# Moving stores, loads and receives between the steps of a one-core decoder kernel, and one layer-norm operand

## The chip, the cores and the metric

The kernel runs on one core of one Trainium2 chip. The metric is the device time of one execution in microseconds. Before the change three runs took 1194.85, 1200.84 and 1200.17 us, a median of 1200.17 us. The work is in float32 throughout.

A core has five engines with an instruction stream each: TensorE (PE, matmuls into PSUM), VectorE (DVE), ScalarE (ACT), GpSimd (POOL) and SyncE (SP). In this kernel nearly all DMA transfers are issued from SP. Each engine carries out its stream in order; semaphores hold an instruction until what it needs is there.

## What is computed

The input is 16 sequences of 128 tokens with 512 features (`x`) and 16 context sequences of the same size. First comes a decoder layer, then a gated cross attention to the same context. Both have 16 heads of 32 features. Cut to what matters:

```python
# decoder layer
ln_out = layernorm(hidden_states, ln1_s, ln1_b)
q, k, v = jnp.split(ln_out @ w_qkv + b_qkv, 3, axis=-1)
x = hidden_states + merge_heads(attention(q, k, v, ltor_mask)) @ w_ao + b_ao
q = layernorm(x, ln2_s, ln2_b) @ w_q + b_q
k, v = jnp.split(encoder_states @ w_kv + b_kv, 2, axis=-1)
x = x + merge_heads(attention(q, k, v, cross_mask)) @ w_co + b_co
x = x + gelu(layernorm(x, ln3_s, ln3_b) @ w1 + b1) @ w2 + b2
# gated cross attention
a = layer_norm(audio_kv, gamma, beta)          # audio_kv is the context
Q, K, V = x @ Wq.T, a @ Wk.T, a @ Wv.T         # 16 heads
out = softmax(Q K^T * scale, masked) @ V
return x + tanh(gate) * (out @ Wo.T)
```

## The kernel before

**Groups and sections.** The 16 sequences are four groups (`GB = 4` sequences each). There are twelve attention sections: A0 to A3 (self attention), B0 to B3 (cross attention to the context) and D0 to D3 (gated). The MLP of the decoder lies between B3 and D0. `x[g]` stays in SBUF for each group.

**Steps.** `attend` (line 634) runs the sections in steps, 16 to a section, four to a sequence. One step handles one unit: four heads (one of each chunk of 128 features) of one sequence. A unit passes through several steps: at step k its scores are scaled and masked (DVE, POOL), at k+1 come the row minimum (DVE) and the exponentials (ACT), at k+2 the normalization (`norm_unit`, POOL), at k+3 the DVE transposes 32x32 blocks and the unit is sent to DRAM (`turn_unit`, tile `away`). Two units make a pair; `receive_pair` (line 581) reads a pair back in four pieces so that the blocks land transposed (tile `pT`). This happens at the start of each even step, two steps after the pair's second unit was sent. When a sequence's two pairs are back, `mix` multiplies with the values (matmuls `av`) at step 4m+2; the first pair has been received four steps before that, the second two. The output projection (`mo`) follows two steps later for A and B. For D0 to D2 it is put off (`deferred`): the mixed values `mT` are kept, in DRAM for D0 and D1 (`put_away`), and multiplied beside the last section.

**What else a step holds.** The `jobs` of a step are pieces of other work, above all the projections of the next section. The dictionary or list that stands beside them says in which step each comes. `ahead.prepare(p)` is work for the section after the next, one call a step. `afterwards(engine, do)` puts a piece off to the start of the next step, where `due()` carries out all such pieces, DVE's first. A piece that puts off another moves that by one step more. All instructions are kept in program order on their engine (class `InOrder`), so the position in the program is the position in the queue, SP's included. All instructions carry line 49 in the profile for this reason; they are told apart by their tiles.

**Turning through DRAM.** Layer-normalized activations are turned in the same manner as the softmax results: DVE transposes blocks, SP sends them to DRAM (`turned_...`), and `receive` (line 254) reads them back in four pieces of 256 KB (`back_...`), two at once and two at the next `due()`. `chunk_back` (ACT) then scales one chunk of 128 features into place.

**Layer norm.** `normalize` (line 206) takes mean and variance (DVE), the inverse root (`rstd`, a 128x1 power on POOL), then, other than at the start, an offset `off = -mean * rstd` of one value per partition (DVE, line 224) and one ACT instruction that scales and shifts. There are 56 such offsets in the program.

**The stages that the change touches.**
- B3 (the last cross group) has as its jobs what `beside_last_cross` (line 1487) lists: the key and value projections of the first gated group with stores of the results (`key_job`, `value_job`), layer norm for the MLP (`mlp_start`, tiles `ln_C`, `turned_C`, `back_C`), twelve loads of MLP weights in pieces of 256 KB, and the first pieces of the MLP.
- The MLP's pieces are numbered by `n` (0 to 16) and `r` (0 to 6). `beside_mlp` adds work for the gated sections, in the last two `n` the preparation of D1 through `gates[1].prepare`.
- In D0 to D3 `GatedAttention.prepare` (line 1300) receives the turned `x` and the turned, normalized context `a` of the section after the next, scales them into place, lets POOL make the sums that the seven-product block multiplication needs (`x_sums`), and, while D0 runs, turns and sends the hidden states of group 3 (`hidden_states`) and adds a term to them (`add_void`).
- Beside D2 `deferred_start` (line 1416) fetches the kept `mT` of D0 and D1 (`mixed`) and the first group's `x` (`x0`), which had been stored to use its place for sums.

**Buffers.** The tag `ln` has one buffer, which `ln_tile` and the received tiles share in turn; `pT` has three; `mT` has one.

Of the kernel before, what the change touches and what calls it, by code (L numbers as in the profile page):

```python
# [25 lines left out]
GB = 4  # L26
# [26 lines left out]
def decoder_then_gated_cross_attention(ctx: ExitStack, tc: tile.TileContext, a: dict, out: bass.AP):  # L53
# [152 lines left out]
    def normalize(src, dst, name, then):  # L206

        mv = work.tile([P, 2], F32, tag="mv", name=f"mv_{name}", bufs=4)
        st = work.tile([P, 6], F32, tag="st", name=f"st_{name}", bufs=4)
        nc.vector.bn_stats(st, src)  # L210
        nc.vector.bn_aggr(mv, st)
        rstd = work.tile([P, 1], F32, tag="rstd", name=f"rstd_{name}", bufs=4)
        nc.vector.tensor_scalar(rstd, mv[:, 1:2], EPS, None, ALU.add)
        nc.gpsimd.tensor_tensor(rstd, rstd, mhalf[:, 0:1], ALU.pow)

        def rest():
            to, of = (by_chunk(dst), squares(src)) if len(dst.shape) == 4 else (dst, src)
            nc.vector.tensor_scalar(to, of, mv[:, 0:1], rstd, ALU.subtract, ALU.mult)
            then()

        def rest_by_act():

            off = work.tile([P, 1], F32, tag="off", name=f"off_{name}", bufs=4)
            nc.vector.scalar_tensor_tensor(off, mv[:, 0:1], -1.0, rstd, ALU.mult, ALU.mult)
            nc.scalar.activation(by_chunk(dst), squares(src), AF.Identity, bias=off, scale=rstd)
            afterwards("dve", then)

        afterwards("dve", rest if at_start[0] else rest_by_act)
# [24 lines left out]

    def receive(name, away):

        t = work.tile([P, NQ, GB, KC, Q], F32, tag="ln", name=f"back_{name}")

        def part(m):
# [3 lines left out]
            )  # L262

        for m in range(2):
            part(m)
# [368 lines left out]
    def attend(sections, ready, others, after=None):  # L634
# [15 lines left out]
        def step(k, bt=None, jobs=(), ahead=None):  # L650
# [10 lines left out]
            if projected and (m == 0 or ready and bt is None):  # L661
                before = projected.popleft()
                if before.sec.deferred:
                    before.sec.put_away(before)
                else:
                    out_project(before)
# [274 lines left out]
    def mlp_start(ml):  # L941
# [17 lines left out]
        def start():  # L959
# [5 lines left out]
        return (  # L965
            ([start, row_difference, lambda: ml_receive(0)], [0, 5, 6]), (sends, [0, 1, 2, 3]), (back, [10, 11, 12, 13])
        )
# [4 lines left out]
    def ml_receive(g):  # L972
        ml.back = receive(f"C{g}", ml.away)

# [3 lines left out]
    def mlp(ml, last_steps):  # L978
# [158 lines left out]
        for n in range(len(steps) + 1):  # L1137
# [6 lines left out]
            if n < len(steps):  # L1144
# [11 lines left out]
                elif g + 1 < NG and i == 2:  # L1156
                    lnT = turned_tile(g + 1)
                    at_[0].append(lambda: ml_receive(g + 1))
                    for c in range(KC):
                        at_[3 + c].append(  # L1160
# [101 lines left out]
    def gated_start(first):  # L1262
# [4 lines left out]
        def key_job(c):  # L1267
            project_chunk(first_k, w["gk"], first.aT, c, "k_D0")
            afterwards("act", lambda: keep_part("k_D0", first_k, c))

        def value_job(b):
            values_chunk(first_v, w["gv"], first.aT, b, "v_D0")
            afterwards("act", lambda: keep_part("v_D0", first_v, b))

# [5 lines left out]
    class GatedAttention(Section):  # L1280
# [19 lines left out]
        def prepare(self, p):  # L1300

            g = self.g
            if g == 2 and p == 0:
                self.ln = ln_tile("D3")
            if g == 2 and p < GB:
                gates[3].hidden_states(p, self.ln[:, p])
            elif g == 2 and p < 2 * GB:
                gates[3].add_void(p - GB)
            if p == 5:
                self.back = receive(f"x{g}", self.x_away)  # L1310
                self.xT = act_tile(self.name, "actT" if g == 3 else "enc")
            elif p in (8, 9):
                self.take_hidden(range(2 * (p - 8), 2 * (p - 7)))
            elif p == 10:
                self.back = receive(f"a{g}", self.a_away)
                self.aT = act_tile(f"a{g}", "actT" if g == 1 else "enc")
                self.x_sides, self.x_sums = right_blocks(self.xT, self.x_at)
            elif p >= 14:
                group_back(self.aT, self.back, "gamma", "beta", range(2 * (p - 14), 2 * (p - 13)))
            if p >= 10 and self.x_sums:  # L1320
# [95 lines left out]
        def deferred_start(self):  # L1416
# [13 lines left out]
            def tokens(g, t):  # L1430
# [7 lines left out]
            return (  # L1438
                ([lambda g=g, n=n: fetch_mixed(g, n) for g in range(2) for n in range(KC)], [6, 7, 8, 9, 10, 11, 12, 13]),
                ([lambda n=n: nc.sync.dma_start(out=x[0][:, n], in_=gated["x0"][:, n]) for n in range(GB)], [8, 9, 10, 11]),  # L1440
                ([begin_sums], [11]),
# [4 lines left out]
        def deferred_jobs(self):  # L1446
# [6 lines left out]
            def product(g, n):  # L1453
# [8 lines left out]
            send = lambda g, b: nc.sync.dma_start(out=out[g * GB + b], in_=x[g][:, b, :])  # L1462
            return (
                ([lambda g=g: add_later(g) for g in (1, 2) for _ in range(4)], [0, 1, 2, 3, 8, 9, 9, 10]),
                *blocks_plan(later, DEFERRED_BLOCKS),
# [21 lines left out]
    def beside_last_cross():  # L1487
# [5 lines left out]
        at_ = [0, 8, 10, 12, 14, 15, 15, 16, 16, 17, 18, 19, 19, 20, 21, 21, 22, 23, 23]  # L1493
        loads = [1, 3, 4, 5, 8, 9, 10, 11, 12, 13, 15, 16]
        return plan(
# [9 lines left out]
    def beside_mlp(n, r):  # L1505
# [17 lines left out]
        elif n == nth - 1 and r == 2:  # L1523
# [4 lines left out]
            sec.take_hidden()  # L1528
            gates[1].prepare(5)
        elif n == nth:  # L1530
# [15 lines left out]
            if r < KC:  # L1546
                project_chunk(sec.q, w["gq"], sec.xT, r, "q_D0", bank="mm0")
            for p in {0: (8, 9, 10), 1: (11,), 2: (12,), 3: (13,), 6: (14, 15)}.get(r, ()):
                gates[1].prepare(p)
# [39 lines left out]
```

## Time and profile before

| what | value |
|---|---|
| median of three runs | 1200.17 us |
| the profiled execution, its own time | 1197.73 us |
| its span, first to last instruction | 1195.9 us |
| mean granted TensorE clock | 0.993 |
| bytes moved by DMA | 253.70 MB, 212 GB/s in the mean |
| TensorE busy, 500 to 600 us (end of B3, start of the MLP) | 90.70 of 100 us |
| TensorE busy, 600 to 950 us (MLP) | 348.82 of 350 us |
| TensorE busy, 950 to 1195.9 us (gated sections) | 228.04 of 245.9 us |

The page lists busy time of each engine. Beside it the trace can be asked for each engine's instructions in order of time. Such a row gives the start in microseconds, the duration, the engine, the operation, the tile written and the tiles read, the shape, the number of instructions merged into the row, and in brackets the idle time in front of it with the instruction that ended it. "SPq" rows are DMA issues; their duration is the issue alone and not the transfer. "PEclk" is the clock that TensorE was granted, as a share of full speed. TensorE's timeline over the MLP and most of A and B shows little idle time; most of it lies in the first 90 us, between 520 and 600 us, and after 970 us.

### The profile page before, as it was taken

To read this page: it belongs to the slowest core of one execution; us is meant where nothing else is said; L and a number is where in the kernel's file an instruction comes from. 1 tells how busy PE (TensorE), PEld (TensorE's weight loads), DVE (VectorE), ACT (ScalarE), POOL (GpSimd) and SP (SyncE) were. 2 spreads that over 40 slices of the span, in tenths; PEclk is the share of its full clock that TensorE was granted. 3 is DMA by queue.
4 is the path that set the end of the run, shared out by engine and by line. 5 is a ranking of instruction groups with operands and counts; after the bars stand their busy time and mean duration, and the time that the engine had idled before them with its cause. 6 is when DMAs were issued, how large, how long until landed. Compare 5 with 4: busy or idle time off the path is not lost.

```text
span 1195.9 us, 21040 instructions
## 1 busy us (share of the span) xinstructions
PE 1152.9 (96%) x7010; PEld 830.0 (69%) x7010; DVE 770.5 (64%) x1493; ACT 593.6 (50%) x2061; POOL 673.4 (56%) x612
## 2 busy tenths in 40 slices
PE   7989999999999999988999999999999989999998
PEld 5867777644444444445788888888888767777775
DVE  7678979776867767865745534453441268777773
ACT  2456767666655656654332233232222238766663
POOL 6778878675757566675223523443342257544873
PEclk9999999999999999989999999999999999999999
DMA  6588979998979979797696494587447718888874
GB/s 213 155 193 212 236 197 217 231 269 200 207 215 206 235 196 242 181 257 221 220 330 193 144 306 152 177 266 263 150 161 247 220 40 230 224 226 239 247 204 159
DMA packets 321796, 253.70 MB, mean 212 GB/s; under 512 B 83156, under 2 KB 279960, under 8 KB 316824
## 3 DMA queue, kind: packets, MB, share of 16 engines
q1 hardware_dynamic: 321648, 252.34, 74.6%
q8 instruction: 56, 0.92, 0.3%
q14 instruction: 52, 0.43, 0.1%
q10 hardware_dynamic: 40, 0.01, 0.0%
HBM read 161.06 MB, written 91.23 MB: 211 GB/s over the span
## 4 chain that ended last, share of the span: by engine, by line
PE 82%; DVE 5%; DMA 4%; POOL 3%; issue 3%; SPq 2%; ACT 1%; ACTq 0%; DVEq 0%; POOLq 0%
PE o L49 15%; PE h L49 14%; PE mo_A L49 5%; PE mm_v_B L49 5%; PE mm_q_B L49 5%; PE mm_k_B L49 5%; PE mo_B L49 4%; PE mm_k_A L49 3%; PE mm_q_D L49 3%; PE mm_k_D L49 3%; PE mm_v_A L49 3%; PE mm_v_D L49 3%; PE mm_o_D L49 3%; PE mm_q_A L49 3%; SPq L49 2%
## 5 line engine op out<-in xcount | busy, mean ns | idle before, releaser
L49 ACT ACTIVATE s_B<-s_B,mn_B 128x128 f32<-128x128 f32 x256 | 99.5, 391 | 78.5 <-issue 59.6
L49 DVE TENSOR_TENSOR h<-h,h 128x512 f32<-128x512 f32 x80 | 54.9, 686 | 114.3 <-PE h L49 113.7
L49 ACT ACTIVATE s_A<-s_A,mn_A 128x128 f32<-128x128 f32 x256 | 99.5, 393 | 52.7 <-issue 37.9
L49 ACT ACTIVATE h<-h 128x512 f32<-128x512 f32 x64 | 40.3, 630 | 156.5 <-DVE h L49 156.5
L49 ACT ACTIVATE s_D<-s_D,mn_D 128x128 f32<-128x128 f32 x256 | 99.5, 391 | 27.1 <-issue 10.6
L49 POOL TENSOR_TENSOR s_D<-s_D,sum_D 128x512 f32<-128x512 f32 x64 | 66.5, 1040 | 76.6 <-DVE sum_D L49 70.8
L49 POOL TENSOR_TENSOR s_B<-s_B,sum_B 128x512 f32<-128x512 f32 x64 | 66.9, 1045 | 62.0 <-DVE sum_B L49 56.3
L49 POOL TENSOR_TENSOR s_A<-s_A,sum_A 128x512 f32<-128x512 f32 x64 | 66.6, 1040 | 52.1 <-DVE sum_A L49 47.3
L49 POOL TENSOR_TENSOR s_B<-s_B,mask 128x512 f32<-128x512 f32 x64 | 81.8, 1278 | 7.6 <-DVE s_B L49 6.0
L49 POOL TENSOR_TENSOR s_A<-s_A,ma 128x512 f32<-128x512 f32 x64 | 81.5, 1274 | 5.9 <-DVE s_A L49 4.3
L49 POOL TENSOR_TENSOR rstd_aD<-rstd_aD,mhalf 128x1 f32<-128x1 f32 x12 | 6.6, 549 | 113.7 <-DVE rstd_aD L49 101.4
L49 POOL TENSOR_TENSOR sh<-h 128x512 f32<-128x512 f32 x32 | 40.7, 1273 | 50.4 <-ACT h L49 43.3
L49 PE MATMUL h<-T_C,w 128*128 128x256 f32 x256 | 61.2, 382 | 2.2 <-DVE h L49 2.2
L49 PE MATMUL mo_B<-w_co,mT_B 128*128 128x512 f32 x128 | 60.7, 618 | 2.5 <-ACT mT_B L49 2.5
L49 PE MATMUL h<-T_C,t 128*128 128x256 f32 x256 | 60.7, 380 | 0.8 <-DVE h L49 0.6
L49 PE MATMUL h<-sx,t 128*128 128x256 f32 x256 | 60.6, 379 | 0.0
L49 PE MATMUL o<-w,h 128*128 128x256 f32 x256 | 60.5, 379 | 0.0
L49 PE MATMUL o<-t,sh 128*128 128x256 f32 x256 | 60.5, 379 | 0.0
L49 PE MATMUL o<-t,h 128*128 128x256 f32 x256 | 60.5, 379 | 0.0
L49 PE MATMUL mo_A<-w_ao,mT_A 128*128 128x512 f32 x128 | 59.1, 604 | 0.0
L49 PE MATMUL mm_v_B<-w_cv,T_e 128*128 128x512 f32 x128 | 57.7, 599 | 0.0
L49 PE MATMUL mm_k_B<-T_e,w_ck 128*128 128x512 f32 x128 | 57.3, 595 | 0.0
(298 smaller groups left out, 2925.0 us busy)
## 6 DMA issues: line engine op xcount, KB each, us to landing
t<-kept SPq DMA_DIRECT2D x24, 1024.0 KB
away_A<-s_A SPq DMA_DIRECT2D x64, 256.0 KB
pT_A<-away_A SPq DMA_DIRECT2D x128, 128.0 KB
away_B<-s_B SPq DMA_DIRECT2D x64, 256.0 KB
pT_B<-away_B SPq DMA_DIRECT2D x128, 128.0 KB
away_D<-s_D SPq DMA_DIRECT2D x60, 256.0 KB
pT_D<-away_D SPq DMA_DIRECT2D x120, 128.0 KB
w<-in_L_xattn_w_dram SPq DMA_DIRECT2D x24, 512.0 KB
```

The source lines that it names most:

```text
L49: return lambda *args, **kw: self.tc.keep_in_program_order(call(*args, **kw))
```

## The change

The layer-norm offset is computed by `tensor_scalar` with `rstd` as a scalar operand, where it was `scalar_tensor_tensor` with `rstd` as a second tensor. All other edits move instructions to other steps:

- `receive` is split: `receiver` makes the tile and hands back a function that issues one piece, so that the caller chooses the step of each piece.
- B3: the pieces of `back_C` go from steps 6, 6, 7, 7 to 7, 9, 9, 10, and the four `chunk_back` from 10 to 13 to 11 to 14; the stores of k and v go from the step after the projection's to an odd step; the twelve weight pieces go from steps 1, 3, 4, 5, 8 to 13, 15, 16 to 1, 3, 5, 7, 11, 11, 13, 13, 14, 15, 15, 16.
- MLP: the four pieces of `back_C` of later groups are issued at r = 0, 0, 1, 1; two of the four sums for D1 go from r = 2 and 3 to r = 5, and two of the four `chunk_back` of its context from r = 6 to r = 5.
- D0 to D2: the pieces of turned `x` are received at steps 1 and 3 (before: 5 and 6), scaled at 5 and 6 (before: 8 and 9); those of `a` at 7 and 9 (before: 10 and 11), scaled at 12 to 15 (before: 14 and 15). `add_void` for group 3 goes from steps 4 to 7 to 8 to 11, and its hidden states are turned in `pT` buffers where an `ln` buffer was used. `put_away` stores `mT` one step later.
- D2, D3: `mixed` is fetched at steps 7, 7, 9, 9, 11, 11, 13, 13 (before: 6 to 13), `x0` at step 15 of D2 and step 1 of D3, two pieces each (before: 8 to 11 of D2).

```diff
-            nc.vector.scalar_tensor_tensor(off, mv[:, 0:1], -1.0, rstd, ALU.mult, ALU.mult)
+            nc.vector.tensor_scalar(off, mv[:, 0:1], rstd, -1.0, ALU.mult, ALU.mult)
...
-    def receive(name, away):
+    def receiver(name, away):
...
+        return t, part
+
+    def receive(name, away):
+        t, part = receiver(name, away)
         for m in range(2):
             part(m)
         afterwards("act", lambda: [part(m) for m in range(2, NQ)])
...
-                    before.sec.put_away(before)
+                    afterwards("act", lambda: before.sec.put_away(before))
...
-            ([start, row_difference, lambda: ml_receive(0)], [0, 5, 6]), (sends, [0, 1, 2, 3]), (back, [10, 11, 12, 13])
+            ([start, row_difference, lambda: ml_receive(0)], [0, 5, 7]), (sends, [0, 1, 2, 3]), (back, [11, 12, 13, 14]),
+            ([lambda m=m: ml.part(m) for m in range(NQ)], [7, 9, 9, 10])
...
-        ml.back = receive(f"C{g}", ml.away)
+        ml.back, ml.part = receiver(f"C{g}", ml.away)
...
                     at_[0].append(lambda: ml_receive(g + 1))
+                    for m in range(NQ):
+                        at_[m // 2].append(lambda m=m: ml.part(m))
...
-            afterwards("act", lambda: keep_part("k_D0", first_k, c))
+            afterwards("act", lambda: keep_later("k_D0", first_k, c, c != 1))
...
-            afterwards("act", lambda: keep_part("v_D0", first_v, b))
+            afterwards("act", lambda: keep_later("v_D0", first_v, b, True))
+
+        def keep_later(key, t, n, wait):
+            if wait:
+                afterwards("act", lambda: keep_part(key, t, n))
+            else:
+                keep_part(key, t, n)
...
-            if g == 2 and p == 0:
-                self.ln = ln_tile("D3")
             if g == 2 and p < GB:
-                gates[3].hidden_states(p, self.ln[:, p])
-            elif g == 2 and p < 2 * GB:
-                gates[3].add_void(p - GB)
-            if p == 5:
-                self.back = receive(f"x{g}", self.x_away)
+                gates[3].hidden_states(p)
+            elif g == 2 and 2 * GB <= p < 3 * GB:
+                gates[3].add_void(p - 2 * GB)
+
+            if p in (1, 7):
+                self.back, self.part = receiver("xa"[p == 7] + str(g), self.a_away if p == 7 else self.x_away)
+            if p in (1, 3, 7, 9):
+                for m in range(2):
+                    self.part(m + 2 * (p in (3, 9)))
+            elif p == 4:
                 self.xT = act_tile(self.name, "actT" if g == 3 else "enc")
-            elif p in (8, 9):
-                self.take_hidden(range(2 * (p - 8), 2 * (p - 7)))
+            elif p in (5, 6):
+                self.take_hidden(range(2 * (p - 5), 2 * (p - 4)))
             elif p == 10:
-                self.back = receive(f"a{g}", self.a_away)
                 self.aT = act_tile(f"a{g}", "actT" if g == 1 else "enc")
                 self.x_sides, self.x_sums = right_blocks(self.xT, self.x_at)
-            elif p >= 14:
-                group_back(self.aT, self.back, "gamma", "beta", range(2 * (p - 14), 2 * (p - 13)))
+            elif p >= 12:
+                group_back(self.aT, self.back, "gamma", "beta", [p - 12])
...
-                ([lambda g=g, n=n: fetch_mixed(g, n) for g in range(2) for n in range(KC)], [6, 7, 8, 9, 10, 11, 12, 13]),
-                ([lambda n=n: nc.sync.dma_start(out=x[0][:, n], in_=gated["x0"][:, n]) for n in range(GB)], [8, 9, 10, 11]),
+                ([lambda g=g, n=n: fetch_mixed(g, n) for g in range(2) for n in range(KC)], [7, 7, 9, 9, 11, 11, 13, 13]),
+                ([lambda n=n: fetch_part("x0", x[0], n) for n in range(2)], [15, 15]),
...
+                ([lambda n=n: fetch_part("x0", x[0], n) for n in range(2, GB)], [1, 1]),
...
-        loads = [1, 3, 4, 5, 8, 9, 10, 11, 12, 13, 15, 16]
+        loads = [1, 3, 5, 7, 11, 11, 13, 13, 14, 15, 15, 16]
...
-            gates[1].prepare(5)
+            for p in (1, 3):
+                gates[1].prepare(p)
...
-            for p in {0: (8, 9, 10), 1: (11,), 2: (12,), 3: (13,), 6: (14, 15)}.get(r, ()):
+            for p in {0: (4, 5, 6, 7, 9, 10), 1: (11,), 5: (12, 13), 6: (14, 15)}.get(r, ()):
                 gates[1].prepare(p)
```

## The prediction, made before the changed kernel was run

> **What bounds the kernel now.** I read the page first, then a table of stretches of 10 us, TensorE's timeline where that table shows it idle, and last the rows of whatever it waits for.
>
> ```profile
> span 1195.9 us, 21040 instructions
> PE 1152.9 (96%) x7010; PEld 830.0 (69%) x7010; DVE 770.5 (64%) x1493; ACT 593.6 (50%) x2061; POOL 673.4 (56%) x612
> ```
>
> TensorE is busy for all but 43.0 us, and the matmuls stay the same, so only idle time and matmuls that a lowered clock stretches can be won. In the timeline (start, duration, operation, idle before it and its releaser):
>
> ```profile
> 65.45 3.54 PE L49 MATMUL mm_q_A<-T_A,sums 128*128 128x256 f32 x8 [3.36 <-ACT q_A L49]
> 68.78 2.04 PE L49 MATMUL mm_q_A<-sums_A,w_sq 128*128 128x256 f32 x8
> ...
> 530.77 1.92 PE L49 MATMUL av_B<-pT_B,v_B 128*32 128x128 f32 x28 [4.16 <-DMA pT_B<-away_B]
> 532.62 5.71 PE L49 MATMUL mm_v_D<-w_gv,T_a 128*128 128x512 f32 x8
> ...
> 984.95 1.12 PE L49 MATMUL sc_D<-k_D__7653,q_D 32*128 32x128 f32 x26 [2.33 <-DVE s_D L49]
> ...
> 1055.27 1.71 PE L49 MATMUL av_D<-pT_D,v_D 128*32 128x128 f32 x28 [2.18 <-DMA pT_D<-away_D]
> 1056.91 4.71 PE L49 MATMUL mm_v_D<-w_gv,T_a 128*128 128x256 f32 x16
> ```
>
> An idle stretch costs twice: the eight matmuls after the first one took 3.54 us, where eight of that shape take 1.89 elsewhere, and the granted clock was 0.83 over 60 to 70 us, 0.66 over 530 to 540 and 0.83 over 1050 to 1060, 1.00 in most others. The two "DMA" waits are for softmax results that went to DRAM and come back turned. The first wait has nothing to do with transfers:
>
> ```profile
> L49 DVE TENSOR_SCALAR rstd_A<-mv_A x16: 153/153/155, 4.7 to 132.5; 128x1 f32<-128x1 f32 x16
> L49 DVE SCALAR_TENSOR_TENSOR off_A<-mv_A,rstd_A x8: 151/824/3428, 46.0 to 135.7; 128x1 f32<-128x1 f32 x8
> ...
> 60.30 3.43 DVE L49 SCALAR_TENSOR_TENSOR off_A<-mv_A,rstd_A 128x1 f32<-128x1 f32 x1 [0.54 <-POOL rstd_A L49]
> ...
> 61.23 1.27 POOL L49 TENSOR_TENSOR s_A<-s_A,ma 128x512 f32<-128x512 f32 x1
> 62.45 1.26 POOL L49 TENSOR_TENSOR sums_A<-sums_A,T_A 128x512 f32<-128x512 f32 x1
> ```
>
> (The first two rows give least, median and longest in ns.) One value per partition took 3.43 us, for as long as POOL ran three tensor operations back to back. ACT's normalization waits for it, ACT's copy of a product out of PSUM (64.48) stands behind that, and TensorE waits for the bank.
>
> **The offset by a scalar operand.** 56 instructions in all: off_A 7.6 us, off_C 11.4, off_aD 4.8, off_B 4.4, off_D 3.1, together 31.3. The nearest row for the new form is the 128x1 TENSOR_SCALAR, 153 to 155 ns each time, POOL busy or not; the next is the 128x512 TENSOR_SCALAR with two scalar operands (ln_A), 534 to 1486 ns, which does stretch beside POOL. I take 0.15: same size, same opcode. At 60.30 the offset is then done at 60.45, ACT's ln_A (0.81) at 61.3 and its copy (0.82) at about 62.2, where TensorE becomes free at 61.95: the idle goes from 3.36 to 0.3 and the 1.65 us of slow matmuls go, **-4.7** (0 if it waits as before, -5.0 at most). Later 2.2 us of TensorE waits for h stand near offsets of 1.22 us in the MLP; half of that, **-1.0** (0 to -2.2). The rest of the 31.3 lies beside a busy TensorE: nothing.
>
> The Trainium skill ("SBUF — State Buffer", Who interferes with whom) says that a DVE instruction with two SBUF inputs contends with POOL, one with a single input doesn't, but that tensor_scalar can enter a two-port mode that does. By its last clause this gain would be 0; by the 153 ns row it is the -4.7 above. That row has no scalar operand from SBUF, so it leaves the point open.
>
> **The last cross group.** Sync's queue issues everything in order, and a receive of four pieces waits for the send of two steps before:
>
> ```profile
> 515.71 2.90 SPq L49 DMA_DIRECT2D pT_B<-away_B  x4
> 518.66 0.43 SPq L49 DMA_DIRECT2D kept_k_D<-k_D  x1
> 519.13 0.98 SPq L49 DMA_DIRECT2D back_C<-turned_C  x2
> 520.22 0.39 SPq L49 DMA_DIRECT2D away_B<-s_B  x1
> ...
> 525.82 1.73 SPq L49 DMA_DIRECT2D pT_B<-away_B  x4
> ```
>
> Counting receives, 515.71 is step 6 and 525.82 step 8. The send at 520.22 stands behind a store of k and two pieces of layer norm; its landing (5.55 us by the chain of waits) releases the receive, and TensorE restarts 4.95 us after that. With the change the stores of k and v, the layer-norm pieces and most weight pieces leave the even steps. Step 4 loses a store and a weight piece: its send goes out after the issue at 507.85, at 508.3 instead of 511.05 (its transpose ended at 506.6), so the receive of step 6 starts 2.7 us earlier, at 513.0. Step 6 loses three issues: send at 515.9. With the old landing of 5.55 the receive of step 8 is at 521.5 and its data there at 526.4; TensorE stops for it now at 526.6. So the 4.16 goes, with the slow matmuls: 28 av in 1.92 against 0.95 (28/32 of 1.08), eight mm_v in 5.71 against 3.60. **-7.2** (0 if only the queue's order changes).
>
> In exchange back_C's fourth piece goes from step 7 to step 10, and ACT reads it in step 11: issued near 527, landed near 531 by the four to five us above, while ACT would come at about 528. Exponentials, POOL's normalization and DVE's transposes queue behind ACT's 3 us. DVE's next step waits for the output projection anyway (2.96 us in front of its x at 543.11), which is the cover; if it is gone this costs the 3 us. I take **+1.5** (0 to 3). The store of the last part of k goes one step later too, and POOL's first weight sum (522.31, after 2.94 idle) seems to wait for its landing; the earlier queue cancels that, 0. The later wait of 2.46 us for mT (549.97) is a loop through TensorE, DVE and ACT and stays.
>
> **The gated sections.** Receives of x move from steps 5, 6 to 1, 3, of a from 10, 11 to 7, 9; stores of mT from 4m to 4m+1. The one long wait is this:
>
> ```profile
> 1043.24 0.91 SPq L49 DMA_DIRECT2D back_x<-turned_x  x2
> 1044.26 0.93 SPq L49 DMA_DIRECT2D away_D<-s_D  x2
> 1051.00 1.74 SPq L49 DMA_DIRECT2D pT_D<-away_D  x4
> ```
>
> The send of step 6 has four back_x pieces around it and lands 6.7 us later; undisturbed ones (1123.61 to 1126.31) take 2.7. With x received by step 3 the receive at 1051.00 comes some 3 us earlier, more than the 2.18 idle: -2.18 - 0.76 (av) - 0.99 (16 mm_v, 3.72 elsewhere) = **-3.9** (0 to -3.9). mixed and x0 on odd steps: **-0.5**, the one short wait near 1119.7. mT has one buffer: its store now leaves after one more send (0.5 us), and ACT's next copy into it comes 4 to 7 us after the issue; landing took about 3. **0** (+4 for eight stores if the margin is gone). The scaling of x and a on ACT and add_void only change places on an engine half idle: 0.
>
> **Start of the gated sections.** Two of POOL's four sums of the second group (1.27 us each) move from r=2 and 3 to r=5 of the last MLP piece, that is, between these two rows:
>
> ```profile
> 968.59 2.88 POOL L49 TENSOR_TENSOR x<-x,u 128x512 f32<-128x512 f32 x2 [3.89 <-DVE u L49]
> 972.70 2.49 POOL L49 TENSOR_TENSOR x<-x,m 128x512 f32<-128x512 f32 x2 [1.23 <-DVE m L49]
> 974.00 0.71 DVE L49 STREAM_TRANSPOSE ln_D<-x 128x512 f32<-128x512 f32 x1 [1.38 <-POOL x L49]
> ```
>
> POOL is free from 971.47 to 972.70, 1.23 of the 2.54; so x and DVE's transpose come 1.3 us later, and DVE, busy without a gap until TensorE's wait at 984.95, hands this on. That wait becomes 3.6. It lowered no clock at 2.33, but 2.18, 2.46 and 3.36 elsewhere did, for about 1.7 us. **+2.2** (0 if DVE's own POOL waits shrink, 3.0 with the clock). The Trainium skill ("TensorE: Matmul & The Clock Gate", Part 1) has the clock fall after an idle window of some 3.4 us that isn't aligned with the program. By it 3.6 would cost the full 3.0; the waits of 2.18 that lowered it here speak for an earlier limit.
>
> **Sum:** -4.7 - 1.0 - 7.2 + 1.5 - 3.9 - 0.5 + 2.2 = -13.6 on the profiled execution's 1197.7: 1184.1. The runs shown go from 1194.85 to 1200.84, and their median, 1200.17, lies 2.4 above the profiled one; I add half, 1185.
>
> **Rivals** (from 1198.9, the same half-way base).
> - *Only the order in the queue changes.* The DMA engines' share was 0.97 and 0.85 over 520 to 540, the bytes stay, and the receive now stands behind odd-step traffic. Then both DMA waits remain: -5.7 + 1.5 + 2.2 = -2.0, **1197**. Against it: in D the queue kept up at 5 us for two steps wherever nothing else was in it.
> - *Slower: the receives that decide come too late.* A receive at steps 0, 4, 8, 12 has two steps until its mix, and the change puts two pieces of 256 KB right ahead at steps 3, 7, 11 and 15: six places in the gated sections. At the mean 212 GB/s that is 2.5 us. Between the last issue and the matmuls lie 4.0 to 4.4 us (1066.77 to 1070.70), and landing took 2.4 to 3.4; it decides once landing exceeds 4.2. Three of six late, 2.5 idle and 1.7 slow each, +12.6; the transfer gains gone: -5.7 + 2.2 + 12.6 = +9.1, **1208**. Against it: the receive itself starts earlier.
> - *The offset still waits for POOL*, as ln_A did: -13.6 + 5.7 = -7.9, **1191**.
>
> **How the numbers follow.** Chances: forecast 0.56 (own range 1178 to 1192), queue order only 0.18, late receives 0.16, offset waits 0.10. Some 0.5%, 6 us, is what a measurement can tell here: faster means below 1194.2. Forecast, most of the third rival and a quarter of the first give 0.68; the rest of the first and edges of the others 0.17; slower 0.15. The range goes from 1177 (all gains, no losses) to 1201, which leaves out most of the late receives and a thin end below.
>
> **What would show it.** Offsets at 0.15 us throughout and no wait near 62; no wait for pT_B at step 10 of the last cross group and no stretched matmuls after it; no wait for pT_D in the second gated section; a later first transpose of the gated sections. Wrong: offsets still up to a microsecond; new waits for pT_D at steps 4, 8 or 12; ACT standing at back_C; a clock drop near 985.

## The result, and the profile after

The changed kernel took 1184.7 us, the median of six executions (1183.69 to 1186.31); six of the kernel before took 1195.75 (1194.57 to 1200.84). The ratio is 0.9898, with a 95% interval from 0.9876 to 0.992: 11 us, or 1.0%, faster. The forecast was 1185. The profiled execution took 1185.11 us, and its page begins:

```profile
span 1183.2 us, 21051 instructions
...
PE 1148.6 (97%) x7010; PEld 828.7 (70%) x7010; DVE 754.2 (64%) x1493; ACT 592.6 (50%) x2061; POOL 673.9 (57%) x612
```

The span is 12.7 us shorter. TensorE is idle for 34.6 us in place of 43.0, and 4.3 us less busy with the same 7010 matmuls. The clock explains only part of that. It was halved for 17.1 us in either profile (before: from 65.7, 529.9, 550.4 and 1055.5 us; after: from 28.1, 540.1 and 973.6), and in that time the matmuls took 16.2 us before and 13.5 after, of which half, some 1.3 us, is the difference that it makes. Where the other 3 us come from isn't shown. DVE is 16.3 us less busy, and the offsets, 31.3 us before, are 11.5 now. TensorE's timeline at the four places shown before:

```profile
64.23 1.97 PE L49 MATMUL mm_q_A<-T_A,sums 128*128 128x256 f32 x8 [0.22 <-ACT q_A L49]
...
523.68 1.08 PE L49 MATMUL av_B<-pT_B,v_B 128*32 128x128 f32 x32
...
975.18 2.04 PE L49 MATMUL sc_D<-k_D__7652,q_D 32*128 32x128 f32 x26 [3.38 <-DVE s_D L49]
977.16 3.60 PE L49 MATMUL mm_q_D<-x,w_gq 128*128 128x256 f32 x8
...
1045.05 1.08 PE L49 MATMUL av_D<-pT_D,v_D 128*32 128x128 f32 x32
```

Three of the four waits are gone or nearly so: 3.36 us became 0.22, and the two mixes (`av`), which had been split into four matmuls, a wait of 4.16 or 2.18 and 28 more, run as one row of 32 in 1.08 us. The fourth grew from 2.33 to 3.38, and the 26 scores and eight matmuls behind it take 2.04 and 3.60 where they took 1.12 and 1.99. Two other waits are longer than in the profile before, one for `rstd_A` near 28 us (2.88, before 0.44) and one for `mT_B` near 541 (3.15, before 2.46). The offsets of the self-attention sections (least, median, longest in ns) and SP's queue between steps 6 and 8, of the last cross group and then of the second gated section:

```profile
L49 DVE TENSOR_SCALAR off_A<-mv_A,rstd_A x8: 204/207/214, 47.9 to 132.2; 128x1 f32<-128x1 f32 x8
```

```profile
511.17 1.89 SPq L49 DMA_DIRECT2D pT_B<-away_B  x4
513.17 0.38 SPq L49 DMA_DIRECT2D away_B<-s_B  x1
...
515.65 0.89 SPq L49 DMA_DIRECT2D away_B<-s_B  x1
517.74 1.74 SPq L49 DMA_DIRECT2D pT_B<-away_B  x4
```

```profile
1034.66 0.38 SPq L49 DMA_DIRECT2D away_D<-s_D  x1
1035.68 2.11 SPq L49 DMA_DIRECT2D back_a<-turned_a  x2
...
1038.99 1.75 SPq L49 DMA_DIRECT2D pT_D<-away_D  x4
```

No offset in the program takes more than 0.22 us now; before, one took 3.43. In the last cross group's queue the send of step 6 stands right behind the receive: 513.17 after 511.17, where it was 520.22 after 515.71. The receive of step 8 follows 4.57 us after that send, where it took 5.60. In the gated section it follows 4.33 us after the send of step 6, where it took 6.74.

To see where the time went I compare stretches of TensorE's timeline: from the first matmul of one group of scores to the first of another ("B 15 to 16" is from the fifteenth to the sixteenth group in the cross sections). An instruction sequence that isn't edited should have the same length in every execution. It often hadn't, which is the main finding of this study. The table holds the profiles of the two kernels and of all others below; a profile with only a part of the edits that act in a stretch is left out of its row. "Without" and "with" mean: without and with the edit that acts in that stretch.

| stretch (us) | without | with | means differ by | predicted |
|---|---|---|---|---|
| A 2 to 3 (offset) | 16.30, 16.30, 18.73, 20.40, 20.43 | 15.63 to 15.67 (9) | -2.8 | -4.7 |
| B 15 to 16 (transfers) | 14.78, 17.04, 17.32, 20.24 | 12.81 to 12.89 (5) | -4.5 | -7.2 |
| B 16 to D 1 (transfers and offset) | 432.90, 433.19, 433.43 | 431.23, 431.44, 431.88 | -1.7 | +1.5 - 1.0 |
| D 2 to 3 (POOL's sums later) | 15.70, 15.72, 17.08, 17.14 | 18.73 to 20.03 (8) | +3.2 | +2.2 |
| D 3 to 9 (receives of x and a) | 73.33, 73.40, 74.74, 75.82 | 71.47 to 71.48 (9) | -2.9 | -3.9 |
| D 9 to 16 (mixed, x0, receives) | 84.07, 84.74, 85.49, 89.25 | 83.18 to 83.20 (10) | -2.7 | -0.5 |
| sum | | | -11.4 | -13.6 |

Where a range is given, the number of profiles stands in brackets. The values without the edits are few and lie up to 5 us apart, so a mean of them, and with it a difference, is uncertain by a microsecond or so. The profile that the prediction was read from has the longest or nearly the longest value in the first two rows and in the fifth, and the shortest in the fourth and the sixth: where it showed a long wait the prediction counted too much, where it showed a short one too little.

### The profile page after: what moved, and what is told of

It is laid out like the page before. It is cut to its first block, busy times and chain, and to the rows that moved or that the text cites. A ratio compares the mean times of both kernels' runs of the same rounds, so it can differ in the third digit from the quotient of the medians.

```text
span 1183.2 us, 21051 instructions
## 1 busy us (share of the span) xinstructions
PE 1148.6 (97%) x7010; PEld 828.7 (70%) x7010; DVE 754.2 (64%) x1493; ACT 592.6 (50%) x2061; POOL 673.9 (57%) x612
## 4 chain that ended last, share of the span: by engine, by line
PE 50%; DVE 1%; ACT 1%; issue 1%; POOL 1%; DMA 0%; SPq 0%; POOLq 0%; ACTq 0%
PE h L49 16%; PE o L49 16%; PE mm_q_D L49 4%; PE mm_v_D L49 3%; PE mm_k_D L49 3%; PE mm_o_D L49 3%; PE sc_D L49 1%; PE av_D L49 1%; PE mo_D L49 1%; PE mo_B L49 1%; POOL x L49 1%; ACT s_B L49 0%; DVE s_D L49 0%; DMA pT_D<-away_D 0%; ACT v_D L49 0%
## 5 line engine op out<-in xcount | busy, mean ns | idle before, releaser
L49 PE MATMUL mm_q_B<-T_B,w_cq 128*128 128x512 f32 x128 | 57.3, 595 | 0.0
```

What stands on the lines that cost most here:

```text
L49: return lambda *args, **kw: self.tc.keep_in_program_order(call(*args, **kw))
```

## The experiments

Times are medians; the ratio to the kernel before, run on the same chip, stands with its 95% interval. The kernel before had medians of 1195.89 (29 executions), 1194.98 (7) and 1194.89 (8) beside the three sets of runs.

**Only the offset.** The kernel before with

```diff
-            nc.vector.scalar_tensor_tensor(off, mv[:, 0:1], -1.0, rstd, ALU.mult, ALU.mult)
+            nc.vector.tensor_scalar(off, mv[:, 0:1], rstd, -1.0, ALU.mult, ALU.mult)
```

> The kernel before with nothing but the offset by a scalar operand. Theory (the offset no longer waits for POOL, and only two places profit): the 56 offsets take 0.2 us each, the idle 3.36 in front of mm_q_A near 65 us falls below 0.5, the third self-attention section begins some 4.7 us earlier, the MLP loses about 1 us of h waits, nothing else moves: 4.7 to 6 us off the 1195.75 of before, 1190 to 1191. Rival (the gains in this change come from the transfers, the offset's wait only changes its place): within 1 us of before. Second rival (DVE was late all along, and all of the 27 us of offset time taken away comes back): more than 8 us off.

1191.67 us, ratio 0.9958 (0.994 to 0.9976): 4.2 us off, a little below the theory's 4.7 (the interval goes from 2.9 to 7.2). Both rivals fall. Its gated sections, which are not edited, took 89.25 us from group 9 to 16, with a wait of 2.60 for `pT_D` that the first profile of the kernel before didn't have.

**Everything but the offset.** The changed kernel with that line turned back.

> The changed kernel with the old offset put back. Theory (the parts add up): the 3.4 us wait near 65 us and the offsets of up to 3.4 us are back, the last cross group and the second gated section stay as in the changed kernel; 1184.7 + 4.7 to 6 = 1189.5 to 1190.5. Rival (the transfers' gain needs the quicker offset, since layer norm for the MLP runs in the last cross group): the transfers' waits come back in part and the time is above 1192.

1189.2 us, ratio 0.9934 (0.991 to 0.9959), 4.5 above the changed kernel, just below the 1189.5 that the theory asked for. The wait near 65 us is back (3.39), the last cross group stays at 12.81. The parts add up.

**Only the last cross group and the MLP's receives.** The kernel before with these, and with the splitting of `receive` that they need:

```diff
-            ([start, row_difference, lambda: ml_receive(0)], [0, 5, 6]), (sends, [0, 1, 2, 3]), (back, [10, 11, 12, 13])
+            ([start, row_difference, lambda: ml_receive(0)], [0, 5, 7]), (sends, [0, 1, 2, 3]), (back, [11, 12, 13, 14]),
+            ([lambda m=m: ml.part(m) for m in range(NQ)], [7, 9, 9, 10])
...
-            afterwards("act", lambda: keep_part("k_D0", first_k, c))
+            afterwards("act", lambda: keep_later("k_D0", first_k, c, c != 1))
...
-        loads = [1, 3, 4, 5, 8, 9, 10, 11, 12, 13, 15, 16]
+        loads = [1, 3, 5, 7, 11, 11, 13, 13, 14, 15, 15, 16]
```

> The kernel before with the edits of the last cross group and of the MLP's receives alone; offset and gated sections as before. Theory (the receive at step 8 was late because of what stood before the send in the queue): no wait of 4.16 us for pT_B and no stretched mm_v_D behind it, 7 us gained by the last section's step 10, ACT stands some 3 us at back_C in step 11, and 5 to 7 us remain: 1189 to 1191. Rival (the gain at step 10 is handed back by the end of the MLP, through the wait for back_C and the one for mT): under 2 us remain, 1194 to 1196.

1190.67 us, ratio 0.9957 (0.9938 to 0.9975): 5.2 off, as the theory had it. But its third group of self-attention scores followed the second 4.1 us sooner than in the first profile of the kernel before, with the same instructions up to there. The offset that had taken 3.43 us at 60.30 took 0.99 here.

**Only the gated sections.** The kernel before with the edits of `prepare`, `put_away`, `hidden_states`' buffers, `mixed`, `x0` and the last piece of the MLP.

```diff
-                    before.sec.put_away(before)
+                    afterwards("act", lambda: before.sec.put_away(before))
...
+            if p in (1, 7):
+                self.back, self.part = receiver("xa"[p == 7] + str(g), self.a_away if p == 7 else self.x_away)
...
-            for p in {0: (8, 9, 10), 1: (11,), 2: (12,), 3: (13,), 6: (14, 15)}.get(r, ()):
+            for p in {0: (4, 5, 6, 7, 9, 10), 1: (11,), 5: (12, 13), 6: (14, 15)}.get(r, ()):
```

> The kernel before with the edits of the gated sections alone (receives of x and a, mixed, x0, stores of mT, add_void, the preparation of the second group at the end of the MLP). Theory (two parts against each other): 3.9 us lost between the MLP's last product and the gated sections' second step, since the two sums on POOL stand in front of DVE's first transpose, 4.2 gained at the wait for pT_D in the second section and 0.5 to 0.9 later: 1195.75 - 1 = 1194 to 1196. Rival (the loss near 980 us belongs to something else, the chip's clock or the shifted phase of the earlier parts): no wait longer than 2.5 us near 985 and 1190 to 1192.

1193.06 us, ratio 0.9973 (0.9955 to 0.9991): 2.8 off, just outside the theory's 1194 to 1196. Its loss is there (idle 3.38, 19.82 us from group 2 to 3), and its gains are 2.9 and 2.7 us by the table and not 4.2 and 0.5 to 0.9. The last cross group, unedited, took 17.32 us and not the 20.24 of the first profile. The three parts alone give 4.2 + 5.2 + 2.8 = 12.2 us, against 11 together.

**The kernel before once more**, without any edit.

> The kernel before once more, for a second profile of it. Theory (its waits for transfers and for the offset differ between executions, and the profile that the prediction was made from showed the long ones): at least two of the four places differ by over 1 us from the first profile (20.40 us for the third group of self-attention scores, 20.24 for the last cross group, 75.8 and 84.1 for the gated sections). Rival (the places are fixed, and the other kernels' profiles differ through their own edits): all four within 0.5 us of the first profile.

All four places differ from the first profile by more than 1 us: 18.73, 17.04, 73.33 and 85.49. The same code waits for a different time from one execution to the next, as the theory had it. What makes a transfer's landing differ isn't shown. For the offset the rows show more. Those of this second profile of the kernel before (DVE's offset, POOL's work beside it, TensorE's wait):

```profile
60.03 3.43 DVE L49 SCALAR_TENSOR_TENSOR off_A<-mv_A,rstd_A 128x1 f32<-128x1 f32 x1 [0.56 <-POOL rstd_A L49]
...
59.97 1.03 POOL L49 TENSOR_TENSOR s_A<-s_A,sum_A 128x512 f32<-128x512 f32 x1
60.97 1.25 POOL L49 TENSOR_TENSOR s_A<-s_A,ma 128x512 f32<-128x512 f32 x1
62.19 1.25 POOL L49 TENSOR_TENSOR sums_A<-sums_A,T_A 128x512 f32<-128x512 f32 x1
...
65.18 1.97 PE L49 MATMUL mm_q_A<-T_A,sums 128*128 128x256 f32 x8 [3.38 <-ACT q_A L49]
```

and those of the kernel with only the last cross group's edits:

```profile
60.04 0.99 DVE L49 SCALAR_TENSOR_TENSOR off_A<-mv_A,rstd_A 128x1 f32<-128x1 f32 x1 [0.56 <-POOL rstd_A L49]
...
59.98 1.03 POOL L49 TENSOR_TENSOR s_A<-s_A,sum_A 128x512 f32<-128x512 f32 x1
```

In both, the offset starts 0.06 us after POOL began a tensor operation. In one it got through when that operation ended, in the other only after POOL's third, when POOL had to wait itself, for DVE. Why it goes one way or the other stays open. Of the five profiles with the old form three show 3.43 us and two 0.99. The new form took 0.21 us there in all nine.

**POOL's sums early.** The changed kernel with the third and fourth sum of the second group back at r = 2 and 3:

```diff
-            if p >= 10 and self.x_sums:
-                nc.gpsimd.tensor_tensor(*self.x_sums.pop(0))
+            if (g > 1 or p in (10, 11)) and p >= 10 and self.x_sums:
+                self.add_sum()
...
+            if r in (2, 3):
+                gates[1].add_sum()
```

> The changed kernel with the second group's third and fourth POOL sums back at r=2 and 3 of the last MLP piece. Theory (these two sums stand in front of the sum that DVE's first transpose waits for): the transpose's wait for POOL falls from 3.0 to about 1.4 us, TensorE's wait for s_D from 3.38 to 2.33, the stretch from the second to the third group of scores of the first gated section from 19.4 to 19.8 us (three profiles with the sums at r=5) to 15.7, 3.5 to 3.9 off 1184.7: 1181. Rival (the loss near 975 us comes from the receives of x at steps 1 and 3 and the hidden states in other buffers): the stretch stays above 19 us and the time at 1184 to 1185.

1182.05 us, ratio 0.9885 (0.9863 to 0.9908), the lowest median of all, though its interval and the changed kernel's overlap and 1181 was expected. First the rows of the changed kernel, then those of this one:

```profile
957.18 2.88 POOL L49 TENSOR_TENSOR x<-x,u 128x512 f32<-128x512 f32 x2 [3.89 <-DVE u L49]
960.02 1.72 POOL L49 TENSOR_TENSOR T_D<-T_D 128x512 f32<-128x512 f32 x1
961.71 1.26 POOL L49 TENSOR_TENSOR x<-x,T_D 128x512 f32<-128x512 f32 x1
962.94 2.49 POOL L49 TENSOR_TENSOR x<-x,m 128x512 f32<-128x512 f32 x2
...
964.23 0.71 DVE L49 STREAM_TRANSPOSE x_D<-x 128x512 f32<-128x512 f32 x1 [3.01 <-POOL x L49]
```

```profile
956.37 2.88 POOL L49 TENSOR_TENSOR x<-x,u 128x512 f32<-128x512 f32 x2 [3.89 <-DVE u L49]
960.48 2.49 POOL L49 TENSOR_TENSOR x<-x,m 128x512 f32<-128x512 f32 x2 [1.23 <-DVE m L49]
...
961.78 0.71 DVE L49 STREAM_TRANSPOSE x_D<-x 128x512 f32<-128x512 f32 x1 [1.38 <-POOL x L49]
...
972.72 1.84 PE L49 MATMUL sc_D<-k_D__7652,q_D 32*128 32x128 f32 x26 [2.33 <-DVE s_D L49]
```

The two sums between `x<-x,u` and `x<-x,m` are the whole difference: 3.01 us of DVE's wait become 1.38, TensorE's 3.38 becomes 2.33. The rival, receives and buffers, falls. The stretch fell to 17.06 us and not to the 15.7 that was expected, since the clock was still lowered (26 scores in 1.84). After waits of 2.33 to 2.35 us here it was lowered in four profiles of six.

**`back_C` early.** The changed kernel with

```diff
-            ([lambda m=m: ml.part(m) for m in range(NQ)], [7, 9, 9, 10])
+            ([lambda m=m: ml.part(m) for m in range(NQ)], [7, 7, 9, 9])
```

> The changed kernel with the pieces of back_C at steps 7, 7, 9, 9 in place of 7, 9, 9, 10. Theory (ACT stood 3.22 us at back_C in step 11 and all behind it came late): that wait is under 0.5 us, the wait of 0.5 for pT_B in front of step 14's mix goes, the 3.15 us for mT falls by 0.5 to 1 and the clock is not lowered behind it: 1 to 3 off 1184.7, 1182 to 1184. Rival (the wait for mT is a loop through TensorE, DVE and ACT which hides ACT's stand): ACT no longer stands, but the wait for mT stays above 2.4 and the time within 0.7 of 1184.7. Slower side: one more piece of 256 KB at step 7 makes the send of step 8 late and a wait for pT_B above 1 us comes back at step 10: 1186 to 1188.

In the changed kernel ACT stood at the first part of `back_C`:

```profile
530.75 0.81 ACT L49 ACTIVATE T_C<-back_C,vcols 128x512 f32<-128x512 f32 x1 [3.22 <-DMA back_C<-turned_C]
```

With the pieces earlier this fell to 0.46 us and the wait for `mT_B` from 3.15 to 2.32. A wait of 1.35 us for `pT_B` came up at step 18 instead, and group 15 to 16 took 13.31 us. From B 15 to D 1 it is 444.34 us against 444.25 in the changed kernel, and the ratio to the kernel before is the same (1183.53 us, 0.9899 from 0.9876 to 0.9923). So the waits were moved and nothing was gained. By its marks this is neither the theory (whose 1 to 3 us didn't come) nor quite the rival (the wait for `mT_B` fell just below its 2.4): that ACT's stand was covered by the wait for `mT_B` is not shown, only that ending it this way brings nothing.

**Both.** The two edits together.

> Both edits together. Theory (they act 430 us apart and add up): 1184.7 - 3.7 - 0 to 3 = 1178 to 1181. Rival (one gain only shifts a wait that the other pays): no better than the better of the two alone.

1182.78 us, ratio 0.989 (0.9867 to 0.9913): no better than the sums alone, as the rival had it.

**Receives at even steps.** In the changed kernel x and a are received at steps 2, 4, 8 and 10:

```diff
-            if p in (1, 3, 7, 9):
+            if p in (2, 4, 8, 10):
...
-            elif p in (5, 6):
-                self.take_hidden(range(2 * (p - 5), 2 * (p - 4)))
+            elif p in (6, 7):
+                self.take_hidden(range(2 * (p - 6), 2 * (p - 5)))
```

> The changed kernel with the receives of x and a in the gated sections one step later, on the even steps 2, 4, 8, 10 (scaled one step later too), everything else as changed. Theory (an even step issues the send that decides, and the pieces of 256 KB beside it make its landing and the next receive late): waits for pT_D of 0.5 to 2.5 us are back in one to three places and the stretch from the third to the ninth group of scores is longer than 71.5, 1 to 4 us lost: 1186 to 1189. Rival (it is not the odd step that counts but that the pieces come two to four steps earlier than before): stretch of 71.5, no waits for pT_D, 1184 to 1185.

1186.34 us, ratio 0.992 (0.99 to 0.9941). The interval overlaps the changed kernel's. But group 3 to 9 took 73.91 us where nine profiles have 71.47 or 71.48, with waits for `pT_D` back in two places, 0.31 us at 1043.09 and this one:

```profile
1050.20 0.93 SPq L49 DMA_DIRECT2D away_D<-s_D  x2
1054.61 1.74 SPq L49 DMA_DIRECT2D pT_D<-away_D  x4
...
1058.64 1.07 PE L49 MATMUL av_D<-pT_D,v_D 128*32 128x128 f32 x28 [1.33 <-DMA pT_D<-away_D]
```

With two pieces of a issued at 1049.19, right ahead of the send, the receive comes 4.4 us after it, and the mix is late. In this profile one step decides.

**Each part of the last cross group turned back**, one at a time in the changed kernel: the pieces of `back_C`, the stores of k and v, the weight pieces.

```diff
-            ([start, row_difference, lambda: ml_receive(0)], [0, 5, 7]), (sends, [0, 1, 2, 3]), (back, [11, 12, 13, 14]),
-            ([lambda m=m: ml.part(m) for m in range(NQ)], [7, 9, 9, 10])
+            ([start, row_difference, lambda: ml_receive(0)], [0, 5, 6]), (sends, [0, 1, 2, 3]), (back, [10, 11, 12, 13])
```

> The changed kernel with the layer-norm pieces back_C where they were (steps 6, 6, 7, 7, scaled at 10 to 13; later groups' second pair at the next due()). The last two groups of scores of the last cross group lie 12.8 us apart in all three profiles with all its edits, 14.8 to 20.2 in the three without. Theory (the pieces around step 6's send are what makes the receive of step 8 late): 14 to 18 us there and a wait for pT_B at step 10, while ACT's stand of 3.22 us at back_C goes: 1185 to 1188. Rival (the queue is what counts and any one of the three parts suffices): 12.8 to 13 us, 1183 to 1185.

```diff
-            afterwards("act", lambda: keep_later("v_D0", first_v, b, True))
+            afterwards("act", lambda: keep_part("v_D0", first_v, b))
```

> The changed kernel with the stores of k and v of the first gated group one step earlier again, on the steps after their projection. Theory (back_C is the main part): a store is one issue of 0.4 us and 256 KB, so 12.8 to 13.8 us between the last two groups of scores and 1184.7 to 1186. Rival (the store, which comes straight ahead of the deciding send, is the main part): over 14.5 us and a wait for pT_B at step 10, 1186 to 1188.

```diff
-        loads = [1, 3, 5, 7, 11, 11, 13, 13, 14, 15, 15, 16]
+        loads = [1, 3, 4, 5, 8, 9, 10, 11, 12, 13, 15, 16]
```

> The changed kernel with the twelve weight pieces at their old steps 1, 3, 4, 5, 8 to 13, 15, 16. Theory (back_C is the main part): the pieces of steps 4 and 8 lie near sends, 12.8 to 14.5 us, and the wait of 0.48 us at step 14 may go, since steps 11 and 13 hold one piece each and not two: 1184 to 1186. Rival (the piece at step 4 delays the send that step 6's receive waits for, and so is the main part): over 14.5 us, 1186 to 1188.

| turned back | median | ratio (95%) | B 15 to 16 | B 15 to D 1 |
|---|---|---|---|---|
| nothing (the changed kernel) | 1184.7 | 0.9898 (0.9876 to 0.992) | 12.81 | 444.25 |
| `back_C` | 1186.39 | 0.9931 (0.9915 to 0.9948) | 14.43 | 445.73 |
| stores | 1185.38 | 0.9921 (0.9906 to 0.9936) | 12.81 | 445.16 |
| weight pieces | 1187.84 | 0.994 (0.9925 to 0.9954) | 12.81 | 447.12 |

Only the weight pieces' interval is clear of the changed kernel's; that the other two lose anything rests on the stretches, and 0.9 us on the stores alone is little: three profiles with all three parts and the new offset have 444.04 to 444.77 from B 15 to D 1. Only `back_C` brings back the wait at step 10 (1.23 us), as the theory had it, while ACT no longer stands at step 11. Without the stores' move ACT stood 4.42 us there. But the weight pieces are worth the most, 2.9 us by the stretch. They act at step 14, where the theory had the short wait going, and after it:

```profile
537.35 1.07 PE L49 MATMUL av_B<-pT_B,v_B 128*32 128x128 f32 x28 [2.12 <-DMA pT_B<-away_B]
541.23 5.85 PE L49 MATMUL mo_B<-w_co,mT_B 128*128 128x512 f32 x8 [2.81 <-ACT mT_B L49]
```

In the changed kernel the first of these waits is 0.48 us, the second 3.15. A wait of 1.19 us at step 18 comes on top, which the changed kernel doesn't have, and ACT stood 4.54 us at step 11. What each of these costs isn't separated. These are single profiles of a place that varies; the medians put the parts in the same order.

## Why the prediction was right, step by step

The mechanisms are right but for the price of ACT's wait, and the time is right to 0.3 us, which is luck. The prediction's base, half-way to the median of three executions, was 1198.9 us, where six gave 1195.75; and its gain of 13.6 us is 11.05 in the medians. Both are too high by some 3 us. Within the sum (-13.6 against the table's -11.4) errors of both signs cancel as well. Two of the four signs that were named for being wrong did come, ACT standing at `back_C` and a lowered clock at the start of the gated sections; the one cost less than was counted for it, the other a microsecond more.

- **The offset, -4.7.** The mechanism is right and the difference between the two profiles is 4.75 us. As a gain of the kernel it is too large: the term was read from an execution in which DVE got through only after POOL's third operation, which two of five didn't do. The means give 2.8. The duration of 0.15 us was 0.17 to 0.22, of no consequence. The doubt drawn from the Trainium skill ("SBUF — State Buffer", Who interferes with whom) is settled for this form by the runs. The same page's sentence that a DVE instruction with at most one SBUF input, outside the two-port modes, doesn't contend agrees with 0.2 us; that the lock goes by issue order doesn't tell why the old form lost it to three POOL operations in a row in some executions.
- **The MLP, -1.0, and ACT's wait for `back_C`, +1.5.** Together +0.5, measured -1.7. ACT stood 3.22 us as described, but no loss of that size is seen: with `back_C` turned back ACT doesn't stand, and B 16 to D 1 is 431.30 us against 431.44; with the pieces early it is 431.03 and 430.89, though there groups 15 to 16 took longer by more than that. The step that failed is this price of 1.5 us, of which 0.1 to 0.6 is seen, and with it the gains behind step 10, which the prediction didn't list: waits at steps 14 and 18 that the kernel before has in some executions (0.74 and 1.60 us in its second profile) and the changed one to 0.48 and none. With the offset alone the stretch is 432.53, with the transfers alone 432.98 and 433.22, with both 431.44.
- **The last cross group, -7.2.** Right to 0.2 us between the profiles (20.24 to 12.81), 4.5 by the means. The queue moved as computed: counted from the start of the kernel before (the stretches ahead are 2.5 us shorter now) the receive of step 6 comes at 513.7 where 513.0 was forecast, the send at 515.7 (515.9), the receive of step 8 at 520.3 (521.5).
- **The second gated section, -3.9,** was 2.9 by the means and 4.35 between the two profiles. The receive that decides starts 4.4 us earlier against the scores ahead of it, where some 3 were forecast. The even steps show, in one profile, that the odd step itself counts and not the earlier receive alone.
- **mixed and x0, -0.5.** This term was mis-sized: 2.7 by the means. The first profile shows one short wait near 1119.7, others waits of 1.45 and 2.60 us. What can be late there was to be seen in it only as a queue with traffic beside every send.
- **The start of the gated sections, +2.2.** The mechanism is right in each step: the sums, POOL's last operation later (by 1.65 us, where 1.3 was forecast), DVE's transpose, TensorE's wait (3.38 against a forecast of 3.6). The size was 3.2, since the wait lowered the clock in all eight profiles that have it, which the prediction only took into its upper end. The sums' return shows it.
- **The rivals.** "Only the queue's order changes" falls with the fixed 12.81 us; the late receives came in none of the nine profiles that have these receives at odd steps; "the offset still waits" falls with 0.2 us. mT's later stores cost nothing: the stretches that hold them have their least values.
- **Not foreseen:** from the first transposed tile to the first scores the changed kernel took 35.47 us, the kernel before 33.66. No instruction there is edited; in the profile it is a wait of 2.88 us (before 0.44) for the `rstd` of layer norm with half the clock behind it. The eight profiles with the offset and all or nearly all of the moves have 33.66 to 35.95 and the six others 33.65 to 34.53. The means are 35.0 and 33.8, so counted in it would bring the table's sum to some -10. Why they differ, and whether by more than chance, stays open.

## What to carry to other kernels

A wait for a transfer in one profile is a draw from a spread: look for it in a second execution before its length goes into a sum, for another may show it longer as well as shorter. Transfers that nothing waits for belong in steps whose sends decide nothing, and the gain is then not only the wait that was seen but every one that might have come. When small operations on an engine with time to spare are moved, look at what stands right behind them in its queue: two sums of 1.3 us cost 3 us here.

## What the runs showed of the hardware

- A DVE instruction on one value per partition with two tensor operands took 0.15 us in the self-attention sections where POOL ran nothing beside it, or only the end of an operation; 0.79 to 1.09 where it got through when the tensor operation under way on POOL ended; and 3.43 where it did so only after three; with the second operand as a scalar the 56 of the program took 0.17 to 0.22 us in all nine profiles. A 128x512 instruction with two scalar operands (ln_A) still took from 0.53 us alone to 1.48 beside a POOL operation in the changed kernel, so it is not the scalar operand alone that frees an instruction from POOL.
- The length of a wait doesn't tell whether the clock is lowered. A wait of 3.36 to 3.39 us near 65 us was followed by slow matmuls in two profiles (3.54 and 3.26 us for eight) and by none in a third (1.97), and waits of 2.33 to 2.35 near 975 lowered the clock in four of six. The Trainium skill ("TensorE: Matmul & The Clock Gate", Part 1) has a window of some 3.4 us that runs free of the program; that the same wait does and doesn't lower the clock agrees with a window that isn't aligned, that 2.33 is enough doesn't agree with a full idle one of 3.4. The traces of this case say more. In each of the 14 profiles the changes of the granted clock lie on a grid of 3.41 us, and the grid begins at another time in each. Counted from the first rise of the clock to the last matmul, in all 31 steps of this grid at full clock in which TensorE was busy for 1.48 us or less the next step had half the clock; of the 18 with 1.49 to 1.87 us four had; above 1.87 none. The wait of 3.38 us that lowered nothing lies across two steps (1.73 and 1.72 us busy), the one of 3.39 in one (0.51 us busy). So the clock goes by the busy time within a step, and the same wait may or may not lower it, by where the grid falls. A step at half the clock costs up to 1.7 us, half its length.
- The stretches of the gated sections between the same groups of scores came out within 0.02 us in nine and ten profiles once the transfers had left the deciding steps, and 2.5 to 5.2 us apart in four before.
